# Layer 1's first sequence begun half by half, the contexts' keys behind the first scores, and another order of layer 0's units

## The chip, the cores and the metric

The kernel runs on one NeuronCore of a Trainium2 chip, as one launch. The metric is the device time of the launch in microseconds (us), lower is better. PE is TensorE (PEld its weight loads), DVE is VectorE, ACT is ScalarE, POOL is GpSimd, SP is SyncE, which here only issues DMAs.

## The reference

A decoder of two layers over 16 sequences of 256 tokens of width 128 in f32, each sequence with a context of 64 rows of width 96. Every block is `x = layernorm(x + block(x))`. Cut to what is computed:

```python
x = ln(x + self_attn0(x))         # 16 heads of 8, causal
x = ln(x + cross_attn0(x, ctx))   # 8 heads of 16
x = ln(x + moe0(x))               # 64 experts, top 6, at most 64 tokens each, plus a shared expert
x = ln(x + self_attn1(x))         # 16 heads of 64, causal, with biases
x = ln(x + cross_attn1(x, ctx))   # 16 heads of 64
x = ln(x + nested_ffn1(x))        # attention, 8 heads of 16, per-quarter widths
# moe0: scores = softmax(x @ gate_w.T); idx = top_k(scores + gate_b, 6)
#   xb[e, pos] = x[token]; h = silu(xb w1) * (xb w3); yb = h w2
#   y[token] += yb[slot] * weight;  z = (silu(x ws1) * (x ws3)) ws2
```

## The kernel before

The program has three stages in time.

**Layer 0** (`contexts` and `layer0(b)`, b = 0 to 15). `contexts` is one program: `context_keys_values` makes the keys (`k0x`, two matmuls of 512 columns) and values (`v0x`, four banks of eight matmuls, each bank followed by eight small copies) of layer 0's cross attention for all sequences; then eight chunks fold layer 1's cross-attention weights with the contexts and store them to DRAM (`gd`, `hd`). `layer0(b)` takes one sequence through self attention (`tp_x`, `qk`, `vp`, scores `s_0a`, `nm_0a`, `p_0a`, ...), cross attention (`s_0x`, ...), the router (`lg`, `sc`, `chosen`, `pos`, `key`, `hit`) and, on POOL, twelve indirect DMAs of 128 rows that scatter its tokens into the experts' slots in DRAM (`xb<-x,slots`).

**Experts.** Eight groups of eight experts: the tokens are read back (`xe<-xb`, only after all scatters), turned (`xet`), multiplied (`eh`, `yp`) and stored (`yb<-ye`). The shared expert runs in eight groups g of 512 tokens: `shared_hidden(g)` makes `hs` (PE `sh`, ACT, DVE), `shared_out(g)` makes `z` and adds it to `x2`; groups 0 to 3 go before the experts, 4 to 7 behind them. The experts' weights `e1, e3, e2` are loaded on SP into the pool `fe`, which opens when layer 0's pools close.

**Layer 1** (`layer1(b)`). POOL gathers each sequence's expert outputs by twelve indirect DMAs (`ge<-yb,slots`), DVE combines them (`xr`, twelve instructions), then layernorm (its power on POOL, `rs_0f`), transposition (`tp_x`, `x3T`), queries, keys and values (`qk`, `vp`), `xpb_1a` on POOL, scores `s_1a`, softmax (`nm_1a`, `p_1a`) and the rest. SP loads the folded weights of a sequence (`gx<-gd`, `hx<-hd`, 1 MB together). The small product `bv_out`, added to `l1_bout`, folds the value bias into the output bias, once.

**What sets the order.** PE, DVE, ACT and POOL run each their instructions strictly in the order in which they stand in their queue. Within layer 0 and within layer 1 that order is written out: each program is recorded as units (neighbouring instructions of one engine), and a string (`ORDER0`, `ORDER1`) names, letter by letter, the program and engine whose next unit comes. Between the separate `manual_schedule` blocks (experts, `bv_out`, layer 1) the compiler's scheduler merges; SP's order it chooses everywhere. A pool that opens on memory of closed pools waits for their last users. Pools lie as a stack; in layer 0 they are, from below, `xt` (with `x2T`, the contexts, the shared expert's weights), `fw` (folding and router tiles, `hit` among them), `kx0`, `x0`. Layer 1's tiles of 4 KB (`v1`, tag `kb4`, 18 buffers) lie on `xt`, `fw` and `fe` and so wait for the shared expert's end.

Of the kernel before, what the change touches and what calls it, by code (L numbers as in the profile page):

```python
# [10 lines left out]
F32 = mybir.dt.float32  # L11
# [23 lines left out]
    ',\'#\'#$#$+$(#)($()*#*))$(*)*)()*))*())*)()*(*()*#*$#*#$**($**(#*)#$%(\'\'$%()\'\')(()*()*(1*)0-#.*((*-**.-(*..(*)#*'  # L35
    '**(///%.(*-/%).(.#/)#/.+.)+/($)-\'/$%.(%\'\'-)\'-./(/./()/--.*#./)(/-)*65/($-*2#)/#/.3(-*$2%).3((442))*-33$43\'\'.4-'
    '-./-./-/.((*/-)(-/)#//+-$/)-\'/.(/2)//%\'3(34-)33*4-)2;:/4.43(-)224242)+4)7.#+3#%34#3+438404$2.0\'4-))27.4%3+8-92'
    '92.%3+8\'3-3-.22/))2+34.4-.+42/23/-47.4-842))+/4#.+4-$-.42\'./324-4-/74.9))%+89\'8+-829.98082.97)+@493-82?7.39-77'
    '.5/87359<9.29#9-.97#.03823908289237984=7$2.7.0433078748293979828497.7.038922937340$<9=79=22978<4932.9.03#9>7>0'
    '=$>%=\'>\'57<938..00=2=7>#382>#3:=#.4.08>730EA%%8<:%=B>$D=\'2\'37<<><><353>A8=7=5>=7>85><>=B9<A>873#9358>C#C%5=B97'  # L40
    'B$<C%<8\'\'=B$C7=<\'\'9<3>35<8=>77>8<85=<9=#>7>$79<>87>A3358>5>=>B:<BC<8#B>73#3>58BC$75<8C$\'9<A>8C%37\'85JAACACA8:='
    '#BBC:BCB<I=CF#CBC?AG=?C<88A%F=CG%:<HFH=#BG:G$<H%G\'\'<H=AA8>8:B=<=:A>ACAB>ABC<C=#CB8C8:<B>AC=<$C:<=\'A=>AC<<A>C=<'
    'BCFC=C%8:8\'GAGH:GGH?AF=CHB88:HG<:OAF=B<HNFF=>GDFGHK=H#HHBD<H=AHF%=?=BGAB?HGAL$?AB\'\'FKHGCFLFM=M=?BBA?CGFCGABHFF'
    'HGHAGC=HF=?BAGAHBFBC?LFHAHAKFLCHBKHGH==?HMLLMA?FBMKLDHLMBLAM=K=?BLAMBK?LLCFLMBMMFKHM=AB?TKMP#MSMKBDGMLFQKPGMDP'
    'LRQKIRKLGIQLFKBBDMGLFKGDLMFMLFGMKQHK$KMBFBDGMKHG#MDK$HFMG#MFLMK$HMPB\'BDMGR%QRD\'QFQFRKGGQHQRFBBFDK#HMRGLD$FK\'PG'
    'RLI%PG\'NPRBFBPRDGPLFQKDYGHLQKNRUGR#RX#LRQ%FGRK%KGPIGL#IQM#QRLIL%K%PMVM$KURG\'G\'ILUWWQKVIPMLPQVV$WV\'\'WQKKLPLMGPG'
    'RIQKRKPQMRPLIQKPRLPR#NRRLUGRGI$RQRIVKVPWPLKVR#LVM#GRGILWPIW$KLWPRU%GI_LQPVUQUNWUWVUWZVNVW#VSW[QSWWPLLUQW$NP$\'\''
    '%UZQW\'\'NV[P]][P^QUULRLNVQPQNURUWUVRUVWPWQZWVPLRLNWUQVPWPWQUQN[UR#WUWVPWP#RWLLNQWPUN]Q%%[S]QPUZQWLLNV[NdP[]U`Q#'
    'VcR[X]#Q]VXP%QU%QSQVZ[aS]$[\'U\'SZVZ[]U][]UV]ZZQQW`S[]VU]ZVSW]U[`WaZ]V]b[bUQZQWS[ZVaa$Sba\'\'b[UUVZVW[Z]U[]UZ[W]ZQ'
    'ZQSV]UZV]S#]]`X$]V][]QQSaUZVbZaSUa#]VaW#$]VbZbUQVSiZe]#bh#V%X[$%Z`[%\'\'Xf^a``[^b`baZb`[VZVXba#[baZXbabZ[b`$]`eb'  # L50
    '\'\'[%ZVgVeX[]#gXaZ]f`%#[a%Zf]`$[\'f\'VgVXfagZZ[`X[]a`b`abZabZ$]b`[\'\'Z`bVVX[`bebXb^ab`b[Zbf`V#bVX[fgZf#Xn[f]`$gm[`'
    'g#$Zbg[je%[^[a$`fe\'\'^eagege^fg#fgcfgac#g[[gf`#a^$g`k\'e%a^%\'`%`aejg[b[#^fkll`a%^eaeb$bf\'a\'e[[e^fgefgegf^`fg`kbe'
    'gaeg``gaea[b[^#g%`^$`ebfgj\'\'ag`kjgaglkcl[k^sealkrkl`keoag`lfaepjfblahjjljlfh`aejoaqcfqkeflckeklefloljkgklaaecf'
    'ljfgclekgpjjfkkegaajcfkelffeckjgkleplpejgljfejlaacfjlloclhlflkqepjfqjalaecpljfgpcpqfjloqkpqaacpeqfjcxooqowqokq'
    'thpmpqffhkqjqpoqkhpuqmjotkqffhpjuvvujhkotpoluvkkjolflofhpoqkqohqjppqjplkqoujqjqkokfoflhqjjohlqkjpqtqkqvmuofvfh'
    'kuuhvjoktuqvpvujoftkhplttvktrvvprjkokmpuopvmuovuvuvopvkqktmpopmtqvouqttpuuotqktkvmptuvoopvtpmutquvooqvtpvovptv'
    'kmktvuvmvvtrptovutpkokmupmqpwuwokkptmmutrutpprrtuvtuuvtpvprurtvuttuuvpprttrvutuwpprutrutuvuptprurwpurwuuwwuuuu'
    'uuwuuwwwwwww'
)
ORDER1 = (  # L60
    '&\'&$&$&&$&$$&$+,#$#+$)#%&#%+#$%$#$%)#%+#%#%#%$+$#%$$#$#)%+#$)#$$%)010$%$&.%+$#$&)%($&#)%$$(&%$%)+%($$&*$$&)#*('
    '%0.(*#*(%%0(%(*(*$$*)&(*))#&)*6)#)%0.(%#0($)#;.5*##%#$5%#$%(.%$$%($&$%)%&$%)&#$*)&3*#0))#+#.%#))%-+%.(%0%*53#*'
    '5(%#*)-$+$(/&-).*)+(/$-*)&#$*(5))#*))**$#*+$%+-/$%-&/$-/$&#/%$(5(*))..#*.(%.+.%$%+#$&)3-&$.#/:3#%-%3#/.5:-$-/3'
    '-.&8-/:($.)(&()*5($*(&*82*:)#)$*-)*)*3+*).+#)./($+/+..(%0(..*(*(0*2*3:#*$2/3(8/:-*..4480(0-.-/)-)&/-/2.3/2+..0'
    '/2)/..(042)/3(3/.30)44(4)*2)*#)4)-$/-$%2$%$2)%2%2.303/-34844:#.8#$#%$#%#$%2$$%73%-8%%%.--./-/-/#/.#.70%./.70/$'
    '8/-8/.09#.#/$0$#%#%#%-%--/-/#//#92%$3#3-4$+43+32+4335(43(&*5$2*(33\'@*5)*/5-)4+)32+.(.42*0(42:7.*3534(843?34-47'
    ')47.389+-39809)5-.+57)/.+795(.7/9)079.(.90-(?)/-2*)/.2/4?(4./)2)*)0*)-?3*.8*87.8(=08?()(*()*()*7)?*7)=*--*8(*='
    '*2=9//3(2*3242)4=24-?433534(3425.4+43=((43(*5)()*2*52*24<024=(4.470.08(<8*9)-=<.=9-88:-.92.8/8:>(842)9:+<>83:3'
    '<>)57=>,E03=58778D92793792988:3929D934<34<>D3<>3<><3>57>88578=9=:-=98=9:-../:./.7D././.--./D-./-8/B22/B<D/<=/B'
    '/<4=7/B447478>29398593797885298-89:34B-2/9:7.48:9--9.D.-/8-:B/-/2/737?979759-93-A/<.5B35=-=7>.5>==<09=.?>=1J7?'  # L70
    '>=?<8<8I>2<>3A==2=>3:2>A?84A>3:CB<CBI7C8A>B7BC==8?>7I89A89AC8:AC8A:C87CI<9==<=B>B2B?>=B>23?343?43<3I434322=432'
    '42I34G7A9G799848:A484GA:4B747G<9G9CIC=<<=><G><>7>==?>2==>?8>2AD4>=<3B?=?2>233:<42>824<4<<>:2>F>8A4G:B7BFC82GCB'
    'B<DCBBD274CB3D78F98F>BGHD<GHHF==:2HA3?G5=AB?A3CACB<6NOAC=FCB<BGCD=CC<N=>HF=>FN=HF=HFHBBADHBGCGA?GCB7=C?78D89D8'
    '98AN8989877B987N9789L<<>LF9FGN9L9F97G>L>A9>H=A7ACB?9C<BC=C8?BBAA=CB<BDC<L>ADCCNB7D78>87CBL7D979<99A=AICACA?C7C'
    '=7K9F8?L=?G7GAH8?HGGF:HGGI8<HIFG;T=<IC=AHS>GGGF<BHBFHIK=HLKDGGHIFBMKGHGDHALKBILHAGLIMGMBMIKBCKSMKBMCKLMB<DMLLD'
    'F==F>S=>K=L>KQK>SL<QHHM<=SF>===<MG<=S><Q>K>ALB>>A>ABF>CQCGCFCFBHAHGDHBHAGDG<BCGGI<AQ>KCI=SLALMQM<LB<N<>=N<=>L<'
    '>PDLFL>FNBH<HHFQDHGIBMGFIFFHL<PDHQ>NHA=FHB<HF=MDHKL?RN=@YXLKKLMFMMXMKLGAGMPBKCILPRMNLGPMLIFQRPMGNLQFQRNRLQGNFG'
    'HXAGHPBPGRIPGRIPRGFXRFHAQHQHQABHXBCBCBKBCKBXCBABCAGMACAGICFBCVICPGCVCFFQCPVPMVRKHQHVFLXVKGSILKKLMKGMKMAMILALUN'
    'GCMBPMLLNMVMILQNALQKRBNBRQQASAACQQASCKCKCKMKMAMMAFUCRGBVFGMAKRBIHQWPQMDSBQKE_SQ^PLPLRPRFRPGNURQQ^ULRKRQQURLVUR'
    'QSVKVWQVNWLWSWKLSMUSLMULWNULWNUWL^UWKVKVMFVMV^MGFMGHGHGF^GHPGHGPGR^FLRPHGHLHFQNHF[KHN[HH[UHL[KKWU[MMK^V[PLXNQP'  # L80
    'PQRFLRRFZPQHNRPQSGRULRQQSR[RNQVSFQVFWFSGGFHFVVPXHHHWFFRPVVXHPWGPPKRFLZRGRNKRVLWKIZLXMPG]]V[JXd[URcVUUcVWPWaWWU'
    'cUWZWQQZ]VVZ]SVVWZXQWPV[SZQ]V[X]P[][XQPXQRcZQRZQ]UQ]SUWQSKW[cULLMLMPLPcVZM[aKM[RLKRKMLKMLKMPLLMaRZQMZMMaSUM[aR'
    ']QcUUWVSUWVUWKQaWVKVPXMWPVV`XWLUaWRVXWKKLLKWVKXMKMUMUMURPWWWUQK^WSK`MLQKbULSZNWQaSLSOi[U[]h]P[`VV`QbX[`b^V]P[['
    'XQP]^U`VQhZR[b[abaaa[Z^Z[]Uf]^]Vh]UVWZVZWh`]V]`bV`bXV`bXZ[b[[Z^[]aU]a^U[aP][f^WWQU^WQRQhRQ`VR`aRPXfWh]QPbQPRPQ'
    'RPQRZVRQXVR[UR`fRUaRPfWPZRhWQf[ZZ[]U]]]Z[[^ZV]PP]cP]QQPX[[PR^e[RV`R^R]fX[V^PaaXPbefURVgZQbaacPbaZacZQZ]XZ]aU]V'
    ']US]ecWQbZVTnmfga`]caZmak``b`mb`be[[beaab^eaabceb[fZcbae[fgZcafgfgg[^gZc[]me[]e[g`[g^`b^[Ubmf`VVWVWUVmaWfVWVUV'
    'UWUVWUVWZkeWkZWefWk]Ugk]`]mW[Wa^U`Wa]``Vb[Zbbk^ba`acZ[baeabcbZf`]acb]UaUcbVVUWUWUW`W`Zbb`[`hbUb^Uj[WeV^k[Uf^`V'
    'g^febffXghVgYsf`fhgrfeaZaegj[gffZhlfgZ[hegj[c]efgfhegagfecfklhZgfkgh[`gja]r[`[][]aer]fabjlfjbahljalckjlkkcjlkk'
    '`rklpa`ZbraZZ][Z]Z[]jr[[]j[ljk]pj]lek]p]pefegefgepgZgrfZf`h]fgfge[hpgZgfhZ[[ZgfZ]hZ]e]e]egegZbgZ`]b[gabZcea[cj'
    'ag^r[_kekll`kf`fmobjkmbkklmpjhlkjm`flkkmlkljoahljkkcolklamelomqofqkqceqkplmafecfg`jagkpmjplp`fl`ahjbaf`khfeeag'  # L90
    'oabaobaofbobpopgpeqpgqfg`qfhqqf`ah`baeb`ab`aoabopbobbep`bqjggk`jbkjljaljlelkkmlk`kljmflclk``bk`mba`abjmbj`llhl'
    '`jfbjlolahfhp`pjqahqppocqparpdelrjpfqropproqkekqqopmofoqgkeqjppmqokqrppfjqrpqkrqjklopklrkmokmkopjpqolpoqoqjljp'
    'prqqpeprqqfoqpfrlpflrokqoqkomqokqfmqoggjjqoggeplpljfrfpokreegepmgfogkgopgmpqegepqgkrpmoprqjpmoqokfqqpgjprjkrol'
    'pqkjfokeqoklkklpjlkrgljkjkljlfjklepelegfrefgkepggerlrljllojepglofkpojjqpoklkoppqpqpopqefqoopqhoqpjqfjpiqjpqqoq'
    'qoqlploolppoqoqoqjqjolkjokqpmopkrnps'
)


class Ref:


    def __init__(self, make):
        self._make, self._made = make, None
# [82 lines left out]
def kernel(ctx: ExitStack, tc: tile.TileContext, a: dict, out: bass.AP):  # L186
# [775 lines left out]
    def widths():  # L962


        for t in (f_nb, f_mask, f_ow, f_ob):
            nc.vector.memset(t, 0.0)
# [325 lines left out]
```

## Time and profile before

| what | value |
|---|---|
| times | 1653.58, 1656.78, 1649.14, 1655.27 us; median 1654.43 |
| profiled execution | 1655.69 us, its span 1653.9 us |
| busy, share of span | PE 90%, PEld 65%, DVE 75%, ACT 67%, POOL 50% |
| layer 0 | 0 to about 598 us (last slots made), scatters to 615 |
| experts, shared expert | 596 to 701 us, overlapping both neighbours |
| layer 1 | first gather at 674, first softmax at 728, end at 1654 us |

All times below are us from the start of the span. Every engine operation is recorded through one helper, so lines all read L141 and groups are told apart by the names of the tiles, without sequence numbers. A row of windows gives, for a stretch, its length, the busy time of PE, PEld, DVE, ACT and POOL (with instruction counts), the granted TensorE clock, the share of the 16 DMA engines and GB/s. A row of the timeline gives start, length, engine, operation, tiles, count and, in brackets, the idle time before and what ended it. A row of the chain gives start, length and what ran.

### The profile page before, as it was taken

What the parts mean: (1) busy time and instruction counts of PE and PEld (TensorE: products, weight loads), DVE (VectorE), ACT (ScalarE), POOL (GpSimd) and SP (SyncE); (2) the same over time, 40 slices, a digit from 0 to 9 for tenths busy, and PEclk for the clock granted to TensorE, in tenths of its full rate; (3) what the DMA queues carried; (4) which work ended last, traced back from release to release, by engine and by line L of the source; (5) the groups of instructions that cost most, each with busy time, mean ns of one, the idle gap of its engine ahead of it and who ended that gap; (6) DMA issues with size and microseconds to landing.
All of it is one profiled execution on the core that took longest, in us unless ns stands there. A gap on an engine that the chain in (4) does not pass through costs nothing.

```text
span 1653.9 us, 36931 instructions
## 1 busy us (share of the span) xinstructions
PE 1485.7 (90%) x12738; PEld 1077.8 (65%) x12738; DVE 1246.3 (75%) x3788; ACT 1107.4 (67%) x3811; POOL 830.7 (50%) x910
## 2 busy tenths in 40 slices
PE   7998989989987678778999999999999999999986
PEld 4665655555555348456777777777778677777764
DVE  5789978978888752345878879868887797788675
ACT  3886778758777321145676778777677767786766
POOL 2144444444444450456827567655666576564441
PEclk9999999989999778779999999999999999999999
DMA  4111110111200057385202232222423322230000
GB/s 141 60 46 34 62 32 27 47 50 37 66 15 2 1 162 198 37 124 51 26 16 29 41 41 36 32 38 17 49 40 44 30 36 40 40 21 5 5 1 11
DMA packets 117190, 73.89 MB, mean 45 GB/s; under 512 B 46555, under 2 KB 106808, under 8 KB 116877
## 3 DMA queue, kind: packets, MB, share of 16 engines
q1 hardware_dynamic: 104717, 58.55, 13.0%
q0 software_dynamic: 12288, 13.00, 11.5%
q8 instruction: 102, 1.67, 0.4%
q14 instruction: 83, 0.68, 0.2%
HBM read 48.05 MB, written 35.65 MB: 51 GB/s over the span
## 4 chain that ended last, share of the span: by engine, by line
PE 44%; DVE 27%; ACT 9%; issue 7%; POOL 6%; DMA 6%; SPq 1%; POOLq 0%; DVEq 0%; ACTq 0%
PE s_1a L141 4%; DMA ge<-yb,slots 4%; PE qk L141 3%; POOL ge L141 3%; ACT p_0a L141 3%; PE o_1a L141 3%; PE s_0a L141 3%; DVE nm_0a L141 3%; PE ptp_1a L141 3%; PE ptp_1f L141 2%; PE pj_1x L141 2%; PE ptp_0a L141 2%; DVE nm_1a L141 2%; DVE x L141 2%; PE vp L141 2%
## 5 line engine op out<-in xcount | busy, mean ns | idle before, releaser
L141 POOL DMA_INDIRECT xb<-x,slots x192 | 189.2, 985 | 258.3 <-DVE hit L141 208.3
L141 ACT ACTIVATE p_1a<-s_1a,nm_1a 128x256 f32<-128x256 f32 (+1 forms) x512 | 211.0, 445 | 68.1 <-DVE nm_1a L141 58.8
L141 POOL TENSOR_TENSOR p_1a<-p_1a,ri_1a 128x512 f32<-128x512 f32 x192 | 197.3, 1039 | 104.5 <-DVE ri_1a L141 90.2
L141 ACT ACTIVATE p_0a<-s_0a,nm_0a 128x256 f32<-128x256 f32 (+1 forms) x512 | 211.7, 453 | 34.5 <-DVE nm_0a L141 34.2
L141 POOL DMA_INDIRECT ge<-yb,slots x192 | 195.6, 1019 | 53.7 <-issue 49.9
L141 ACT COPY pT_1a<-ptp_1a 128x512 f32<-128x512 f32 x192 | 105.9, 619 | 56.7 <-PE ptp_1a L141 56.3
L141 DVE TENSOR_REDUCE nm_1a<-s_1a 128x2 f32<-128x512 f32 (+1 forms) x192 | 126.1, 673 | 19.2 <-PE s_1a L141 19.2
L141 DVE TENSOR_REDUCE nm_0a<-s_0a 128x2 f32<-128x512 f32 (+1 forms) x192 | 125.0, 683 | 11.3 <-PE s_0a L141 11.0
L141 PE MATMUL qk<-x3T,l_wqkv 128*128 128x256 f32 x512 | 126.0, 388 | 2.8 <-DVE r1a L141 1.4
L141 ACT ACTIVATE p_1f<-s_1f,nm_1f 128x256 f32<-128x256 f32 x256 | 119.8, 507 | 11.5 <-DVE nm_1f L141 11.2
L141 PE MATMUL ptp_0a<-ident,p_0a 128*128 128x128 f32 x768 | 111.0, 280 | 13.7 <-ACT p_0a L141 8.1
L141 ACT ACTIVATION_READ_ACCUMULATOR p_0a<-s_0a,nm_0a 128x1 f32 x512 | 122.0, 238 | 0.0
L141 ACT COPY pT_0a<-ptp_0a 128x512 f32<-128x512 f32 x192 | 106.5, 617 | 21.9 <-PE ptp_0a L141 21.5
L141 ACT ACTIVATION_READ_ACCUMULATOR p_1a<-s_1a,nm_1a 128x1 f32 x512 | 117.7, 230 | 0.0
L141 PE MATMUL ptp_1a<-ident,p_1a 128*128 128x128 f32 x768 | 100.8, 275 | 11.1 <-POOL p_1a L141 7.3
L141 DVE SCALAR_TENSOR_TENSOR xr<-ge,slot_w,xr 128x128 f32<-128x128 f32 x160 | 61.0, 381 | 64.1 <-DMA ge<-yb,slots 60.7
L141 PEld LDWEIGHTS qk<-x3T,l_wqkv 128*128 128x128 f32 x512 | 95.2, 196 | 19.9 <-issue 6.1
L141 PEld LDWEIGHTS ptp_0a<-ident,p_0a 128*128 128x128 f32 x768 | 85.7, 142 | 33.7 <-ACT p_0a L141 20.6
L141 PE MATMUL s_1a<-kT,qT 64*128 64x256 f32 (+1 forms) x1024 | 101.4, 339 | 5.2 <-ACT p_1a L141 5.0
L141 PE MATMUL o_1a<-pT_1a,v 128*64 128x128 f32 x1536 | 97.1, 278 | 3.3 <-ACT p_1a L141 1.2
L141 PEld LDWEIGHTS ptp_1a<-ident,p_1a 128*128 128x128 f32 x768 | 87.1, 142 | 16.1 <-POOL p_1a L141 8.9
L141 PEld LDWEIGHTS o_1a<-pT_1a,v 128*64 128x64 f32 x1536 | 85.4, 139 | 18.5 <-issue 3.4
(258 smaller groups left out, 3686.8 us busy)
## 6 DMA issues: line engine op xcount, KB each, us to landing
gd<-g1x_sb SPq DMA_DIRECT2D x32, 256.0 KB
hd<-h1x_sb SPq DMA_DIRECT2D x32, 256.0 KB
gx<-gd SPq DMA_DIRECT2D x16, 512.0 KB
hx<-hd SPq DMA_DIRECT2D x32, 256.0 KB
xb<-x,slots POOLq DMA_INDIRECT x192, 2.2
ge<-yb,slots POOLq DMA_INDIRECT x192, 4.2
e<-in_w1T SPq DMA_DIRECT2D x8, 352.0 KB
e<-in_w3T SPq DMA_DIRECT2D x8, 352.0 KB
```

The lines of the kernel that those rows point to most:

```text
L141: r = f(*[made(x) for x in a], **{n: made(x) for n, x in k.items()})
```

## The change

1. **Start.** The first sequence's tokens and `l0_wqkv` are loaded first; the clearing of `xb` (2 MB of zeros) and of `yb`'s last row moves from SP into ACT's queue; the contexts and their weights come next, the shared expert's weights last. In `ORDER0` PE's queue begins with the first sequence's `tp_x`, then `k0x`'s first matmul, `qk`, `vp`, `k0x`'s second, the first scores, and then the four `v0x` banks; before it began `k0x, k0x, v0x, tp_x, v0x, qk, vp, v0x, scores`. SP fetches the tokens one or two sequences further ahead.
2. **`ORDER0`.** Beyond the start, units are exchanged with near neighbours in many places on all four engines, more of them towards the end. At the end PE now has the last sequence's transposition `tp_x` (of `x1`) ahead of the sequence before's `pos`, and behind that `pos` only the last sequence's 14 remaining units; before, `lg` and `pos` of the sequence before stood ahead of that transposition.
3. **Pools.** `fw` becomes one of layer 0's own pools, so `fe` lies on `fw`, `kx0` and the foot of `x0`; before it lay on `kx0` and `x0`. `v2` (gathers) and `vaf` open with the experts, on the right side; `vaf` is cleared on DVE in `widths` instead of on POOL behind the experts.
4. **Layer 1's first sequence.** One manual block holds everything from the experts on. The gathers of sequence 0 come first, `bv_out` and its addition into the shared expert's tail, then sequence 0 in two halves of 128 tokens: combine, norm, turn, queries, keys and values of each, with matmuls and evictions of 128 columns instead of 256.
5. **`ORDER1`** is, on every compute engine, the old order with the units that item 4 took out missing at its front (PE 13, DVE 17, ACT 10, POOL 7); five neighbouring pairs on DVE are exchanged, and on SP the loads of one more sequence stand ahead.

```diff
-    ctxT = load("ctxT", ...)
-    fw = pool_of(phase_ab, name="fw", bufs=2)
-    ws1 = load("ws1T", ...)
...
     with ExitStack() as phase_a:
+        fw = pool_of(phase_a, name="fw", bufs=2)
...
+        tokens0 = tokens(0)
         l0_wqkv = load("l0_wqkvT", [D, 3 * D], pool=x0_pool)
+        nc.scalar.dma_start(
+            xb.rearrange("(s p) d -> p s d", p=P),
+            zero.unsqueeze(1).to_broadcast([P, NSLOT // P, D]),
+        )
+        nc.scalar.dma_start(yb[NSLOT : NSLOT + 1, :], zero[0:1, :])
+        ctxT = load("ctxT", [DC, B, KV], pool=xt_pool)
...
+    vaf = [wc.tile([P, 2, 8, 32], F32, tag=f"vaf_{i}", name=f"vaf_{i}") for i in range(2)]
+    v2 = pool_of(name="v2", bufs=2, side="right")
...
+    def normed_half(b, i, x, r):
...
+        nc.vector.bn_stats(st, r[:, i, :])
+        nc.vector.bn_aggr(mv, st)
+        nc.vector.tensor_scalar(mv[:, 1:2], mv[:, 1:2], EPS, None, ALU.add)
+        nc.gpsimd.tensor_tensor(rs, mv[:, 1:2], neg_half[:, 0:1], ALU.pow)
+        nc.vector.tensor_scalar(x[:, i, :], r[:, i, :], mv[:, 0:1], rs, ALU.subtract, ALU.mult)
...
+    bv = value_bias()
+    gathered(0)
+    hs5 = shared_hidden(5)
+    shared_out(4, hs4)
+    hs6 = shared_hidden(6)
+    shared_out(5, hs5)
+    hs7 = shared_hidden(7)
+    add_value_bias(bv)
+    r_0 = combine(0, (0,))
...
+    normed_half(0, 0, x_0, r_0)
+    shared_out(6, hs6)
+    turned_half(0, 0, x_0, xT_0)
+    shared_out(7, hs7)
     phase_ab.close()
...
+    queries_of(0, 0, x_0, xT_0, *qkv_0)
+    combine(0, (1,))
+    normed_half(0, 1, x_0, r_0)
+    turned_half(0, 1, x_0, xT_0)
+    queries_of(0, 1, x_0, xT_0, *qkv_0)
```

`queries_of` makes, for one half, four banks of four matmuls of 128 columns, evicts eight blocks on DVE (`qT`) and eight on ACT (`kT`), and two banks of 512 columns for the values, one copied by ACT and one by DVE. `turned_half` is one transposition and one copy; `combine` is the old loop of six instructions per half.

## The prediction, before the run

> **What bounds the kernel now.** I read the windows by stage first, to see where engines are idle at all, since a change of order can only win idle time.
>
> ```profile
> 0.00:20.00 20.00, 12.50 (x66) 8.19 (x70) 8.07 (x31) 2.24 (x4) 9.46 (x30) 1.00 0.73 209
> 200.00:300.00 100.00, 88.35 (x781) 54.74 (x779) 84.47 (x308) 73.64 (x276) 43.51 (x49) 0.97 0.11 32
> 560.00:600.00 40.00, 19.33 (x70) 9.64 (x70) 26.35 (x132) 6.50 (x17) 19.25 (x21) 0.62 0.13 33
> 690.00:705.00 15.00, 6.37 (x26) 5.81 (x27) 6.14 (x16) 0.00 (x0) 4.88 (x5) 0.50 0.48 38
> 705.00:735.00 30.00, 21.06 (x110) 15.15 (x108) 14.52 (x39) 10.51 (x36) 15.08 (x16) 0.78 1.05 137
> 1200.00:1400.00 200.00, 192.51 (x1762) 151.74 (x1759) 158.86 (x441) 148.43 (x503) 126.36 (x137) 1.00 0.31 39
> ```
>
> From 800 us on PE is busy 94 to 97%; that stretch keeps its order, and I expect it only to shift. In the middle of layer 0 PE (88%) and DVE (84%) bind together. Idle time lies at four places: the start (PE idle 7.5 of 20 us, ACT nearly wholly), layer 0's end (PE 20.7 of 40), and 690 to 735, where PE is idle 17.6 of 45 us and ACT sleeps. The chain of waits says who ends each.
>
> ```profile
> 4.47 2.68 DMA l0x_wk<-in_l0x_wk
> 7.20 3.78 PE k0x L141 x4
> 10.98 1.91 PE v0x L141 x16
> 12.88 0.62 PE tp_x L141 x2
> ...
> 689.53 6.37 issue
> ...
> 701.93 4.97 issue
> ...
> 720.85 12.92 DMA ge<-yb,slots
> ```
>
> At the start the contexts' weights and matmuls stand ahead of the first sequence. At the turn of the layers the chain runs through POOL's gathers: POOL stands 6.37 us (for sequence 0's last gathers, behind its power) and 4.97 us (`xpb_1a`, behind `bv_out`), and then DVE waits for gathers in flight. Third, the timeline at three places.
>
> ```profile
> 22.03 0.37 ACT L141 ACTIVATE p_0a<-s_0a,nm_0a 128x128 f32<-128x128 f32 x1 [0.56 <-DVE nm_0a L141]
> ...
> 567.51 0.23 PE L141 MATMUL pos<-chosen,upper 128*128 128x64 bf16 x1 [5.75 <-DVE chosen L141]
> ...
> 594.23 0.34 SPq L141 DMA_DIRECT2D e<-in_w1T  x1
> ...
> 720.05 2.06 PE L141 MATMUL s_1a<-kT,qT 64*128 64x128 f32 x32
> ...
> 727.67 0.35 DVE L141 SCALAR_TENSOR_TENSOR xr<-ge,slot_w,xr 128x128 f32<-128x128 f32 x1 [0.98 <-DMA ge<-yb,slots]
> 727.94 1.28 DVE L141 TENSOR_REDUCE nm_1a<-s_1a 128x4 f32<-128x512 f32 x2
> ```
>
> The first exponential runs at 22.03. The last sequence's chain stands behind a `pos` that waits 5.75 us. Layer 1's scores are there at 720 to 725, but its first softmax waits for 727.67: the last gather of sequence *1*, whose combination stands before it on DVE.
>
> **Start.** The tokens' issue moves from 7.30 to about 0.8; landing then took 3.0 us (`xpb_0a` at 10.33), so `tp_x` starts at about 3.8 instead of 12.8, and `xT` is there at about 5.5 (DVE's 1.77 us cast stands before it until then). `k0x`'s first matmul is now queued between `tp_x` and `qk` and waits for `l0x_wk`: issued fourth, at about 2.2, landing 2.68 later, so 4.9 if undisturbed, some 2 us later beside the zeros. It costs half of 3.78 us, 1.9. `qk` then runs from about 7.5, and from `xT` to the first exponential there were 7.8 us (14.23 to 22.03), of which 1.1 was a `v0x` bank before `qk`: the first exponential comes at about 14, 8 us earlier. That is not all won. Up to 33 us PE was busy 23.2 us (12.5 of the first 20, and 10.7 in the windows after), and the same work started at 3.8 cannot end before 27: at most 6 us earlier. Between 8 (if ACT's softmax decides) and about 2 (if PE stalls on the contexts) I take 5, near the PE sum's end, because PE is busy 36 of the 40 us from 20 to 60.
>
> ACT now issues the zeros. On SP the second of these issues lasted 5.28 us, which ACT will be held for, to 8 or 10 us; its first work (`kx`) is due at about 9. Cost 0 to 1, taken 0. A rule speaks against this move: the Trainium skill ("DMA: Bandwidth & Descriptors", Issuing engines are not separate DMA queues) says that DMAs of SP, ACT and POOL run on the same 16 DMA engines and interleave. By it the zeros share the engines with the first loads instead of following them; the row of 0 to 20 us, DMA share 0.73, leaves room. If all 2 MB stood ahead of the contexts, the gain at the start would be near 0 instead of 5; the zeros' issue behind two loads makes that the far end.
>
> **Layer 0's order.** At the end, `pj_0a` of the last sequence finishes at 561.2, its `x1` needs 0.3 (`r0a`), 0.9 of statistics, 0.74 on POOL and 0.6, so 564 to 564.5; it came at 567.97, behind the sequence before's router on DVE and its `pos` on PE. That exchange is worth up to 3.6 us; I take 3, since the delayed router must still end before the last scatters. The other exchanges can't be priced one by one. PE is idle some 53 us between 60 and 560 (by the windows), in waits of 1 to 6 us; one exchange moves a wait of this size either way. I take 0, with 8 down (a sixth of the idle) and 8 up.
>
> **Pools.** The experts' weights were issued at 594.23, just after `sb` (593.77 and 0.29) read the last tile of `x0`; `fe` now also covers `fw`, whose last user is the last `hit` at 600.3: 6 us later. About 6.6 MB follow at full DMA share until 619.4, then `xe` is issued, and PE takes up `xet` at 622.3. If the weights shift by 6, `xe` queues behind them: cost 5.5. If SP issues layer 1's 2 MB of weights, which don't lie on `fw`, in the gap, cost 0. The compiler chooses SP's order and has already put constants ahead (the loads at 19.9 us); I take 2. `vaf` on DVE is under 1 us where DVE is busy 12.83 of 46: nothing.
>
> **Turn of the layers.** The last `yb` store is issued at 671.25 and gathers start at 674.14 as before. PE's tail without waits: `sh` to 684.1 as now, then `bv_out` (16 records; 3.75 at half clock, 1.9 at full) to 686. DVE: the first half's six combinations 686.5 to 688.2, statistics to 689; the power waits until POOL has issued all twelve gathers (689.53), so the first half is normed at 690.8. Last `z` at 693.1; that frees `v1` (701.3 before). The first half's queries: 8 DVE and 8 ACT evictions of some 0.35, the value copies 0.6 and 0.7: to 697.7. Second half's combination and norm 3.7, turning 0.7, queries again 4.5: 706.5, instead of 718.7 with `vp`'s copies. The scores come about 13 us earlier. Added are 8 DVE and 8 ACT evictions, about 2 us on each; they lie in this stretch, where ACT was busy 0.00 of 15, and cost nothing; without that cover, 2.
>
> But the first softmax still stands behind sequence 1's gathers. POOL is in order: it can start these only after the second half's power, at about 701, and then needs 12 x 1.305 and `xpb_1a` 0.72: issue ends at 717.5, as before (717.9). Before, the last landed 9.7 us after its issue, because `gx` and `hx` (1 MB per sequence, four sequences) held the DMA engines from 701 to 735 (share 1.05). They now start when `v1` is free, at 693, and end some 8 us earlier. The last gather lands between 722 (lag as at 708) and 728 (12 at the contended 1.86 us each, from 707). I take 726.5; the next gathers (sequence 2's, awaited until 733.8) gain about as much. Turn: 2.5 won, from 3 lost to 8 won.
>
> On the clock: it was granted at 0.50 from 688 to 709, after PE's idle stretches. The Trainium skill ("TensorE: Matmul & The Clock Gate", HAM oscillation) asks for no idle gap over 3.4 us; the new gaps are by my list 2.9 and 4, so part of the halves would run slow, for perhaps 2 us, hidden behind the gathers.
>
> **Sum**, against the profiled execution's 1655.69 (span 1653.9 and 1.8 around it; 1.3 above the median): start -5, end of layer 0 -3, other exchanges 0, weights +2, turn -2.5: -8.5, so 1647.2, and 1645.9 on the median. I say 1646.
>
> **The rivals.** (1) *The wins are absorbed*: PE's lead from the start is lost in layer 0's in-order waits, the weights come the full 6 us late, and the gathers land when they did: -5 -3 +5.5 -0 leaves 2.5 won, 1652. For it: the chain passes POOL and DMA, not PE. Chance 0.21. (2) *All wins carry through*: 8 at the start, 3.6 at the end, 6 by the exchanges, 8 at the turn: 1629. For it: idle time of that size is there. Against it: DMA at share 1.05. Chance 0.12. (3) *Slower*: the new order of layer 0 fits other durations than the chip's, and units placed early wait at the head of PE's and DVE's queues. Place: 60 to 560 us, where waits of DVE on ACT and of PE on DVE are 0.5 to 6 us. It decides once it adds more than the 8.5 won and the 5 of measurement, a quarter on the 53 us of idle; with 20 added, 1666. For it: some 150 of 694 places in PE's queue hold another unit. Against: most are swaps of neighbours. Chance 0.15. The forecast has 0.52.
>
> **Numbers.** About 0.3% (5 us) is what a measurement of this kernel can tell from no change: faster is below 1649.4. The forecast's own range, 1639 to 1653, lies about four fifths below this (0.42); with rival 2 (0.12) and a third of rival 1's spread (0.08), 0.62 faster. Same gets the rest of both, 0.23; slower 0.15. The range for 8 in 10 leaves out about 0.08 below and 0.12 above: 1635 to 1660.
>
> **What would show it.** Right: first exponential at 13 to 16; last `slots` 6 to 10 us before 597.5; first `s_1a` about 12 us earlier against the last `yb` store, but first `nm_1a` only 1 to 4 us earlier against it. Wrong: `xet` over 30 us behind the last `slots` (24.8 now), more PE idle than 53 us between 60 and 560, or `nm_1a` directly behind the scores.

## The result, and the profile after

The change makes the kernel slower by a little: 1657.5 us (median of 42 runs, 1653.2 to 1662.6) against 1652.5 for before in the same series (69 runs). The ratio is 1.0031, with a 95% interval of 1.0023 to 1.0038, so 5.1 us, 3.8 to 6.3. The forecast was 8 us the other way. The profiled execution after took 1659.70 us, its span 1657.4 (before 1655.69 and 1653.9).

The windows of after, in the stretches shown of before (length, busy time of PE, PEld, DVE, ACT and POOL, granted clock, DMA share, GB/s):

```profile
0.00:20.00 20.00, 10.51 (x74) 6.51 (x76) 7.99 (x23) 5.02 (x20) 9.46 (x30) 1.00 0.70 205
200.00:300.00 100.00, 88.08 (x757) 55.30 (x755) 86.25 (x307) 74.81 (x279) 45.27 (x49) 0.97 0.11 35
560.00:600.00 40.00, 22.27 (x158) 12.87 (x159) 25.31 (x119) 11.53 (x33) 18.72 (x21) 0.70 0.05 10
690.00:705.00 15.00, 10.52 (x53) 9.21 (x53) 7.04 (x21) 3.20 (x9) 1.80 (x3) 0.77 0.92 120
705.00:735.00 30.00, 13.40 (x93) 10.33 (x93) 9.37 (x28) 4.55 (x10) 17.36 (x18) 0.74 1.07 117
1200.00:1400.00 200.00, 194.39 (x1784) 153.50 (x1783) 160.07 (x441) 144.91 (x491) 124.47 (x135) 1.00 0.29 38
```

The halves do fill 690 to 705 (PE busy 10.52 of 15 us, 6.37 before, ACT 3.20 instead of 0.00), but the 30 us after it are emptier by more than that: PE 13.40, before 21.06. Late in layer 1 (1200 to 1400) PE is as full as before: 194.39 of 200 us, before 192.51. The chain of waits (start, length, what ran) says what stands at the start and at the turn:

```profile
2.38 6.73 DMA l0x_wk<-in_l0x_wk
9.25 2.04 PE k0x L140 x2
...
692.13 14.66 issue
722.67 12.48 DMA ge<-yb,slots
```

`l0x_wk` now lands in 6.73 us instead of 2.68, beside the zeros, although fewer bytes were issued ahead of it on SP (704 KB, before 1032). At the turn, POOL stands 14.66 us in one piece ahead of the second half's power, and then the chain goes through the last gather of sequence 1. The timelines of the engines (start, length, engine, operation, tiles, and in brackets the idle time before and what ended it) show what that does:

```profile
17.52 0.37 ACT L140 ACTIVATE p_0a<-s_0a,nm_0a 128x128 f32<-128x128 f32 x1 [0.58 <-DVE nm_0a L140]
...
706.84 0.55 POOL L140 TENSOR_TENSOR rsh<-mvh,neg_half 128x1 f32<-128x1 f32 x1 [14.70 <-DVE mvh L140]
...
716.12 2.06 PE L140 MATMUL s_1a<-kT,qT 64*128 64x128 f32 x32
...
735.24 0.35 DVE L140 SCALAR_TENSOR_TENSOR xr<-ge,slot_w,xr 128x128 f32<-128x128 f32 x1 [1.43 <-DMA ge<-yb,slots]
735.51 1.28 DVE L140 TENSOR_REDUCE nm_1a<-s_1a 128x4 f32<-128x512 f32 x2
...
739.19 1.11 PE L140 MATMUL ptp_1a<-ident,p_1a 128*128 128x128 f32 x4 [17.58 <-POOL p_1a L140]
```

The first exponential comes at 17.52 (22.03 before, 14 forecast). Layer 1's first scores come at 716.12, earlier than before, and then stand 19 us: the first reduce is directly behind sequence 1's last sum of gathered rows, and PE is idle 17.58 us in one piece. Set against the first gather (676.09 after, 674.14 before), the scores come at 40.0 us (45.9 before), but the first reduce at 59.4 (53.8).

In layer 0 the times of `slots` give the lead of the new order at each sequence's end: 4.0 us at the first (85.5, before 89.5), 3.1 at the second, and 1.5 us *behind* at the third (162.4, before 160.9); 2.9 behind at the last (600.4, before 597.5). These are single profiles, and they differ by some us: a second one of the same kernel (e15 below) has the first slots at 82.0, the third at 158.2 and the last at 598.0; it lacks a stretch of half clock, 6.8 us at 50 us, that the first has. In both, about 5 us of the lead are lost between the first slots and the third (5.5 and 4.8).

### The profile page after: what moved, and what is told of

It reads as the page before. It is cut to its first block, busy times and chain, and to the rows that moved or that the text cites. A ratio compares the mean times of both kernels' runs of the same rounds, so it can differ in the third digit from the quotient of the medians.

```text
span 1657.4 us, 37019 instructions
## 1 busy us (share of the span) xinstructions
PE 1482.1 (89%) x12770; PEld 1076.6 (65%) x12770; DVE 1254.8 (76%) x3801; ACT 1111.6 (67%) x3819; POOL 829.7 (50%) x909
## 4 chain that ended last, share of the span: by engine, by line
PE 46%; DVE 25%; ACT 10%; issue 7%; POOL 5%; DMA 5%; SPq 0%; POOLq 0%; DVEq 0%; ACTq 0%
PE s_1a L140 5%; DMA ge<-yb,slots 4%; PE qk L140 4%; ACT p_0a L140 4%; PE s_0a L140 4%; PE o_1a L140 3%; POOL ge L140 3%; PE ptp_1a L140 3%; PE ptp_0a L140 3%; PE ptp_1f L140 2%; DVE x L140 2%; PE pj_1x L140 2%; DVE nm_0a L140 2%; PE s_1x L140 2%; DVE nm_1a L140 2%
## 5 line engine op out<-in xcount | busy, mean ns | idle before, releaser
L140 PE MATMUL qk<-x3T,l_wqkv 128*128 128x256 f32 (+1 forms) x544 | 128.5, 381 | 1.9 <-DVE r1a L140 0.8
L140 PEld LDWEIGHTS qk<-x3T,l_wqkv 128*128 128x128 f32 x544 | 98.7, 202 | 17.8 <-issue 4.9
L140 PEld LDWEIGHTS ptp_1a<-ident,p_1a 128*128 128x128 f32 x768 | 87.4, 142 | 27.2 <-POOL p_1a L140 20.5
L140 POOL TENSOR_TENSOR p_1x<-p_1x,cri_1x 128x512 f32<-128x512 f32 x64 | 66.0, 1045 | 59.6 <-DVE cri_1x L140 40.8
```

What stands on the lines that cost most here:

```text
L140: r = f(*[made(x) for x in a], **{n: made(x) for n, x in k.items()})
```

## Experiments

Three theories. **A**: the loss is in layer 0's new order. **B**: it is at the turn of the layers, where sequence 1's gathers wait for the second half's power. **C**: the start is won nowhere, because the zeros take it back. A difference between two variants below is the difference of their ratios to before, times 1653 us; its uncertainty is the root of the summed squares of the half intervals.

### Taking the change apart: four kernels

`e1_turn_alone`: the kernel after with layer 0 as before.

```diff
-    tokens0 = tokens(0)  ...  nc.scalar.dma_start(xb, zero)  ...  ctxT, l0x_wk, l0x_wv
+    ctxT, ws1, ws3, ws2  ...  l0_wqkv, l0_wout, ...   (old order of loads)
+    contexts(): clear_slots() on nc.sync first
-    ORDER0 = new
+    ORDER0 = old
```

> The kernel after with layer 0 as it was before: the loads at the start in their old place and order, the two clears of the rows on SP's queue again, and the old ORDER0. New are then only the pools and the turn of the layers (sequence 0 half by half, value bias early) with the new ORDER1. Theory A (the loss of the change sits in layer 0's new order): this is faster than before by what the turn was priced at, about 2.5 us, ratio 0.998 to 0.9995. Theory B (the loss sits at the turn, where sequence 1's gathers wait for the second half's power and lie beside the loads of gx and hx): slower by 3 to 5 us, ratio 1.002 to 1.003, with the first nm_1a as far behind the last yb store as in the kernel after (63 us, 57 before). Theory C (the two profiles differ by chance and both parts are near nothing): 0.9995 to 1.0005.

Measured: 1.0014 (0.9998 to 1.0030), 2.3 us lost, 2.6 either way. The turn, with the pools and the new `ORDER1`, does not win its 2.5 us; between the first gather and the first reduce lie 58.9 us here, as in the kernel after.

`e2_layer0_alone`: the kernel before with the loads, the clears on ACT and the `ORDER0` of after.

> The kernel before with layer 0 as it is after: tokens, projections, contexts and key weights loaded first, the clears on ACT's queue, the new ORDER0; the turn of the layers, ORDER1 and the place of fw stay as before. Theory A: the new layer 0 ends later by the 2.9 us that the profile after shows at the last slots, and that carries: ratio 1.0015 to 1.0025. Theory B: layer 0 ends within 1 us of before on the average of the runs, ratio 0.9995 to 1.0005. The on-record sum had it 8 us earlier (start 5, end 3): ratio 0.995.

Measured: 0.9999 (0.9986 to 1.0013). The new layer 0 as a whole wins nothing of its 8 us. And the kernel after, which adds the turn to it, is 5.3 us slower (2.6 either way). So both A and B hold something.

`e3_new_start_old_order` and `e4_old_middle` cut `ORDER0` (2460 units on the four compute engines) at two places where both orders have handed out the same units:

```diff
 # e3: units of ORDER0
   0 to 166: new          # the start, to about 40 us
-  166 to 2460: new
+  166 to 2460: old
 # e4
   0 to 166: new
-  166 to 2049: new
+  166 to 2049: old       # about 40 to 520 us
   2049 to 2460: new      # the end of layer 0
```

> The kernel after with its first 166 units of layer 0 (the start, up to about 40 us) and then the old order of units to the end of layer 0. Against the kernel e1 it differs by the start alone. If an in-order schedule carries a start that is 4 us earlier (first exponential at 17.5 instead of 22.0), it is 3 to 4 us faster than e1, and the slots of the sequences stand 3 to 4 us earlier to the end. If the start's gain is used up by something that does not depend on the order (the transfers of the first 60 us), it is within 1 us of e1 and the lead is gone by the third sequence (161 us).

Measured: 0.9982 (0.9967 to 0.9997); against e1, which has the old start, 5.3 us won (3.6 either way). The last slots come at 590.5 (595.4 in e1). The start's gain carries to the end; theory C falls.

> The kernel after with only the middle of ORDER0 put back: the first 166 units and those from the 2050th on stand as in the kernel after, the units between (about 40 to 520 us) as before. If the new middle costs the 5 to 8 us that the profile shows between the first sequence's slots and the thirteenth's, this is the fastest of the four layer-0 variants, 5 to 8 us faster than the kernel after (ratio to before 0.998 to 1.000). If the new tail alone is worth the 4 us that the profile after regains past 545 us, it is 4 us faster than e3; if that regain is only sequences waiting less after a late middle, it equals e3.

Measured: 0.9970 (0.9957 to 0.9982): 2.0 us below e3 (3.2 either way, so the end alone is not told from nothing), and 10.1 us below the kernel after (2.5 either way). So the four parts are: start 5.3 won, end 2.0 won, middle of layer 0 10.1 lost, turn 2.3 lost. That they add up to the 5.1 measured is by construction, each being the step between two kernels of one row.

### The turn: what stands behind what

`e5_half_gathers_first` uses POOL's idle 14.7 us:

```diff
     normed_half(0, 0, x_0, r_0)
+    gathered(1, (0,))          # six gathers of sequence 1's first 128 tokens
     shared_out(6, hs6)
...
-        gathered(b)            # layer 1, sequence 1: all twelve
+        gathered(b, (1,) if b == 1 else (0, 1))
```

> The kernel after with six of sequence 1's twelve gathers (its first 128 tokens, whose buffer is free once sequence 0's first half is combined) put on POOL ahead of the power of sequence 0's second half, so that they go out in POOL's idle time between 692 and 707 us. If sequence 0's first reduce (nm_1a) waits behind sequence 1's sums of gathered rows on DVE, as the trace after shows (PE idle 17.6 us from 721.6), the last gather goes out about 7 us earlier, and nm_1a follows by 4 to 7 us: ratio to before 0.9995 to 1.001, where the kernel after has 1.0031. If the transfers of gx and hx set when the gathers land (1.8 us apart whatever their issue), nm_1a moves by under 2 us and the time by under 1 us: 1.0025 to 1.0035.

Measured: 0.9988 (0.9975 to 1.0001), 7.1 us below the kernel after (2.5 either way), somewhat more than expected. POOL's timeline and DVE's:

```profile
692.41 1.06 POOL L140 DMA_INDIRECT ge<-yb,slots  x1 [0.18 <-issue]
...
706.70 0.57 POOL L140 TENSOR_TENSOR rsh<-mvh,neg_half 128x1 f32<-128x1 f32 x1 [6.68 <-DVE mvh L140]
...
725.27 0.35 DVE L140 SCALAR_TENSOR_TENSOR xr<-ge,slot_w,xr 128x128 f32<-128x128 f32 x1 [1.94 <-DMA ge<-yb,slots]
725.54 1.28 DVE L140 TENSOR_REDUCE nm_1a<-s_1a 128x4 f32<-128x512 f32 x2
```

The power of the second half is where it was (706.70), six gathers went out before it from 692.41, and the first reduce comes 10 us earlier, still behind the same sums. Sequence 0's transposed `x4T` comes 104.3 us behind the first gather (113.9 after, 109.1 before).

`e6_gx_hx_held` takes the loads of `gx` and `hx` out of the gathers' way:

```diff
-    nc.sync.dma_start(gx, ...)
+    nc.sync.dma_start(gx, ..., then=behind sequence 1's twelve gathers)   # sequences 0 to 3
```

> The kernel after with the loads of gx and hx of sequences 0 to 3 held until sequence 1's twelve gathers have landed; the gathers are issued from the same place as in the kernel after, in program order just behind the power of the second half. If the gathers land late because those 4 MB lie on the same DMA engines, they land 2 to 3 us behind their issue instead of 12.5 and nm_1a comes at about 726 instead of 735.5: 5 to 9 us gained there, ratio to before 0.998 to 1.001, unless gx of sequence 0 is then late for its scores (needed at about 775, loaded by about 745: it should not be). If the gathers are paced by their own packets, no change: 1.0025 to 1.0035.

Measured: 1.0024 (1.0009 to 1.0039), 1.2 us below the kernel after (2.8 either way), so the second theory's numbers. DVE's waits for gathered rows:

```profile
729.12 0.35 DVE L140 SCALAR_TENSOR_TENSOR xr<-ge,slot_w,xr 128x128 f32<-128x128 f32 x1 [1.13 <-DMA ge<-yb,slots]
730.98 0.35 DVE L140 SCALAR_TENSOR_TENSOR xr<-ge,slot_w,xr 128x128 f32<-128x128 f32 x1 [1.50 <-DMA ge<-yb,slots]
...
750.77 0.35 DVE L140 SCALAR_TENSOR_TENSOR xr<-ge,slot_w,xr 128x128 f32<-128x128 f32 x1 [6.59 <-DMA ge<-yb,slots]
```

With no other load beside them the gathers still land 1.5 to 1.9 us apart (1.6 to 2.5 in the kernel after). The last lands 4.3 us earlier, at 730.98, 9.2 us behind its issue (12.5 in the kernel after); 0.9 of the 4.3 is that here it is issued ahead of `xpb_1a`, at 721.78 instead of 722.67. But the held loads then lie beside sequence 2's gathers, for which DVE waits 6.59 us in one piece (3.78 in the kernel after), and the 4.3 us are given back. The contention is real but small, and moved rather than removed.

`e7_seq0_first_round_ahead` and `e8_seq0_two_rounds_ahead` change only places in `ORDER1`:

```diff
 # DVE's queue; PE, ACT and POOL likewise
-  sums of sequence 1's rows (4 units), sequence 0's reduces and reciprocals
+  sequence 0's first 8 units (e7) or 16 units (e8), sums of sequence 1's rows
```

> The kernel after with one change in ORDER1: sequence 0's first eight units on DVE (with those of PE, ACT and POOL between them) stand ahead of sequence 1's first unit on DVE, which is the sum over its gathered rows. So nm_1a of sequence 0 no longer waits for sequence 1's gathers. Theory B in its sharper form (the earlier scores win nothing because the next step stands on DVE behind sequence 1's gathers): first nm_1a at 717 to 718 instead of 735.5, PE's idle stretch of 17.6 us shrinks to under 8 in one piece, and 3 to 8 us are gained at the end: ratio 0.998 to 1.001. If sequence 1 is what the following steps wait for, whatever sequence 0 does, the gain is under 2 us: 1.002 to 1.003.

> As the run before it, but with both of sequence 0's rounds of scores (16 units on DVE) ahead of sequence 1's sums. If DVE has time to spare until sequence 1's rows have landed (735 us), this is at least as good as the smaller move: 0.997 to 1.001. If the sums and with them the gathers of sequence 2 (they wait for the buffers that the sums set free) come too late, it gives some of that back: 1 to 4 us slower than the smaller move, with DVE's waits for gathered rows at 750 to 775 us longer.

Measured: e7 1.0024 (1.0008 to 1.0039), 1.2 us below the kernel after; e8 0.9992 (0.9981 to 1.0003), 6.4 us below (2.3 either way). DVE's first reduce and PE's next long wait, in e7 and then in e8:

```profile
718.98 1.29 DVE L140 TENSOR_REDUCE nm_1a<-s_1a 128x4 f32<-128x512 f32 x2 [1.61 <-PE s_1a L140]
740.58 0.66 PE L140 MATMUL tp_x<-ident,x 128*128 128x128 f32 x2 [14.71 <-DVE x L140]
```

```profile
714.42 1.29 DVE L140 TENSOR_REDUCE nm_1a<-s_1a 128x4 f32<-128x512 f32 x2 [1.61 <-PE s_1a L140]
736.50 0.66 PE L140 MATMUL tp_x<-ident,x 128*128 128x128 f32 x2 [12.62 <-DVE x L140]
```

In both the first reduce is 17 us closer to the first gather than in the kernel after, directly behind its scores. In e7 that is worth nothing: PE then waits 14.71 us for sequence 1's normed rows, since behind the first round its queue holds sequence 1's units. In e8 PE still waits 12.62 us there, but more of sequence 0 is done by then (PE busy 48.6 of the 50 us from 740, 44.1 in the kernel after). So my sharper form of theory B is half right: an earlier first softmax alone wins nothing; what counts is when sequence 1's rows come, or how much other work is placed ahead of them.

### The middle of layer 0, and a faster version

`e9_old_first_part`: the kernel after with units 166 to 716 of `ORDER0` (about 40 to 162 us) old, all others new.

> The kernel after with ORDER0's units 166 to 716 (about 40 to 162 us, the end of the third sequence's slots) put back as before, and the rest new. The whole old middle (units 166 to 2049) made the kernel after about 10 us faster. If the loss sits in the first sequences (the profiles: 77.0 us from the first to the third slots, 71.4 with the old middle, part of it a dip of the granted clock), this wins 4 to 6 us of it: ratio to before 0.9995 to 1.001. If it is spread evenly (per unit), it wins 29%, about 3 us: 1.001 to 1.002. If it sits behind, under 1 us: 1.0025 to 1.0035.

Measured: 0.9987 (0.9973 to 1.0001), 7.3 us below the kernel after (2.6 either way). That is more than the 4 to 6 expected for a loss in the first sequences: most of the middle's 10 us lies in this stretch, 29% of its units.

`e10_middle_and_gathers` is e4 and e5 together, `e11_and_seq0_ahead` adds e8's places, `e12_old_turn_new_ends` is the kernel before with e4's layer 0.

> The old middle of ORDER0 (as in e4_old_middle, ratio 0.997) together with six of sequence 1's gathers ahead of the second half's power (as in e5_half_gathers_first, 4 us below the kernel after). They lie in different stages. If both carry, 4 us below 0.997: 0.994 to 0.995. If layer 1 sets its own pace from the first gathers on, the second gives 0 to 2 us: 0.996 to 0.997.

> e10_middle_and_gathers and, besides, both of sequence 0's rounds of scores ahead of sequence 1's sums on DVE (as in e8_seq0_two_rounds_ahead). Both edits remove the same wait of nm_1a for sequence 1's gathers, so the gains do not add: within 2 us of e10, ratio 0.993 to 0.996. If sequence 1 is then late (its sums stand behind 16 units of sequence 0), up to 3 us slower than e10.

> The kernel before (its turn of the layers, ORDER1 and place of fw) with the new start and the new end of ORDER0 and the old middle, that is the layer 0 of e4_old_middle. Against e4 it differs by the turn alone. With the new turn priced at 2.3 us lost (e1) to 5 us lost (the kernel after against e2), it is 2 to 5 us faster than e4: ratio 0.994 to 0.996. If the turn is near nothing, 0.9965 to 0.9975.

Measured: e10 0.9934 (0.9917 to 0.9951), e11 0.9930 (0.9912 to 0.9948), e12 0.9941 (0.9921 to 0.9961). e10 is 6.0 us below e4 (3.5 either way): the two gains are of different stages and both carry. e11 is level with it, as expected of two cures for one wait. e12 against e4 prices the new turn once more, at 4.8 us lost (3.9 either way). With its gathers reordered (e10) the new turn is no worse than the old one, and not measurably better either. e10, 1643.0 us where before took 1654.2, beats both kernels by 0.7% (before) and 1.0% (after).

### Waits or clock?

In the profile of after, this first part of the middle looks like this at its worst place: PE's two waits, then the windows around them.

```profile
154.22 0.33 PE L140 MATMUL tp_x<-ident,x 128*128 128x128 f32 x1 [1.41 <-DVE x L140]
...
157.63 2.07 PE L140 MATMUL s_0a<-kx,qT 32*128 32x512 f32 x2 [1.78 <-DVE x1T L140]
```

```profile
153.00:155.00 2.00, 0.78 (x4) 0.67 (x7) 1.94 (x5) 2.00 (x8) 1.75 (x2) 1.00 0.11 29
155.00:157.00 2.00, 0.84 (x6) 0.01 (x1) 1.83 (x9) 0.16 (x1) 1.80 (x3) 0.86 0.01 0
157.00:159.00 2.00, 1.37 (x2) 0.50 (x2) 2.00 (x5) 0.80 (x5) 0.08 (x1) 0.50 0.38 125
159.00:161.00 2.00, 2.00 (x11) 1.12 (x11) 1.00 (x5) 0.71 (x5) 0.00 (x0) 0.50 0.52 203
```

DVE is full (1.94 and 1.83 of 2 us), PE is busy 1.62 of 4 us, and the granted clock falls to 0.50 from 156.4 to 163.2. What DVE is full with is not another order: from the fourth sequence's `x1` over the third's router (`sc` to `chosen`) to the copy `x1T` its instructions are the same, in the same order, as before. What moved is on POOL, as the rows of after and then of before show:

```profile
152.03 2.13 DVE L140 TENSOR_SCALAR x<-r0a,mv_0a,rs_0a 128x128 f32<-128x128 f32 x2
153.01 1.06 POOL L140 TENSOR_TENSOR kx0x<-kT0x,hm 128x512 f32<-128x512 f32 x1
```

```profile
152.98 0.60 DVE L141 TENSOR_SCALAR x<-r0a,mv_0a,rs_0a 128x128 f32<-128x128 f32 x2
155.38 1.38 DVE L141 TENSOR_TENSOR chosen<-rp,sb 128x128 bf16<-128x128 f32 x1
155.53 1.06 POOL L141 TENSOR_TENSOR kx0x<-kT0x,hm 128x512 f32<-128x512 f32 x1
```

The new order has `kx0x` and `xpb_0x` one scatter earlier in POOL's queue, and so `kx0x` runs beside DVE's two `x`, for which PE's `tp_x` waits; before, it ran later, beside `chosen`. The second `x` lasts 1.87 to 1.88 us in all eleven profiles with this stretch of the new order and ends about 0.1 us behind `kx0x`; in the nine with the old stretch it lasts 0.34 or 0.35. The 242 DVE instructions that in before ran from 85 to 161 us take 81.5 to 82.1 us in the eleven, 79.1 to 79.4 in the nine. No run exchanges these POOL units alone, so what this one exchange costs is not shown.

The dip of the clock begins 69 to 74 us behind the first slots in the profile of each kernel with this stretch that does not fill the wait, and in none of those with the old stretch and the new start. (e1, with the old start, has a short one at 68 us.) It was open whether the waits or the clock cost the 7 us. `e13_filled_wait` puts work of no use into the first wait; `e14_new_first_part_alone` puts the new stretch into e10.

```diff
     def transposed(x, dst, name, fill=0):
         for i in range(2):
+            for _ in range(fill if i else 0):       # fill=6 for sequence 3's x1
+                nc.tensor.matmul(t[:, 2 * P : 3 * P], ident, ident, start=True, stop=True)
             nc.tensor.transpose(t[:, i * P : (i + 1) * P], x[:, i, :], ident)
```

> The kernel after with six matmuls of no use (identity by identity, 128 columns, about 0.28 us each) ahead of the second transpose of sequence 3's x1, where PE waits 1.41 us for DVE at about 153 us. Clock theory (a few us with PE mostly idle make the granted clock fall to half from 156.7 to 163.2 us, and that costs some 3 us): the clock stays at 1.00 there, first to third slots take 73 to 75 us instead of 76.2 to 77.0, ratio to before 1.001 to 1.002. Wait theory (the clock follows something else, and the loss is the waits): the dip stays, the stretch takes 76 to 77.5 us, ratio 1.003 to 1.0035. The second gap, 1.78 us at 155.8, is not filled; if that alone is enough for the dip, the wait theory's numbers come out too, and the run does not tell them apart.

> The fastest version (e10_middle_and_gathers, 0.9934) with ORDER0's units 166 to 716 as in the kernel after and the other middle units as before. If this stretch costs 7 us whatever surrounds it: ratio 0.9970 to 0.9980, first to third slots 76 to 79 us with a dip of the clock in them. If its price came only with the rest of the new middle: 0.993 to 0.995.

Measured: 1.0098 (1.0070 to 1.0125) and 1.0014 (0.9994 to 1.0035), on a chip where before took 1686 us. There PE stands 20.5 us (e13) and 17.9 us (e14) in waits for nothing that the profile shows; 2.4 to 3.0 in all other profiles. Neither has its base on that chip, so the times settle nothing; in e13's profile the dip is gone. I ran both again, each beside its base.

> The kernel after, unchanged, as the base for the filled wait on this chip. Expected: its ratio to before as over all its runs, 1.002 to 1.004, with a dip of the granted clock 70 to 80 us behind the first slots and 76 to 78 us from the first to the third slots.

> The kernel after with the six matmuls of no use in PE's wait at about 153 us, beside its base. Clock theory: the dip 70 to 80 us behind the first slots is gone, the stretch is 2 to 3 us shorter, and the time is 1 to 3 us below the base (ratio lower by 0.001 to 0.002). Wait theory: no dip is removed, or it is removed without gain; the time is that of the base or up to 2 us above it (the six matmuls last 1.7 us at full clock).

> The fastest version (old middle of ORDER0, six of sequence 1's gathers first), unchanged, as the base for the next run. Expected: 0.992 to 0.995, first to third slots 71.5 us without a dip (75 with one).

> The fastest version with ORDER0's units 166 to 716 as in the kernel after, beside its base. If this stretch costs the same 7 us whatever surrounds it: ratio above the base by 0.003 to 0.005, first to third slots 76 to 79 us. If its price came only with the rest of the new middle: within 0.0015 of the base.

Measured: e15 1.0028 (1.0010 to 1.0045), e16 1.0010 (0.9988 to 1.0032), e17 0.9932 (0.9911 to 0.9954), e18 0.9959 (0.9940 to 0.9978). The windows of e15, of e16 and of e17, from the first slots on and around the dip:

```profile
82.00:158.00 76.00, 64.53 (x544) 39.18 (x543) 64.41 (x222) 51.35 (x191) 34.63 (x37) 0.95 0.13 41
150.00:162.00 12.00, 10.60 (x41) 7.07 (x42) 9.76 (x35) 5.57 (x21) 5.14 (x6) 0.57 0.16 55
```

```profile
82.00:158.00 76.00, 65.77 (x575) 41.62 (x574) 65.22 (x230) 53.62 (x198) 34.62 (x37) 1.00 0.13 41
150.00:162.00 12.00, 10.19 (x77) 5.95 (x77) 11.53 (x41) 7.63 (x28) 5.65 (x7) 1.00 0.16 55
```

```profile
82.00:158.00 76.00, 68.28 (x595) 42.00 (x594) 66.74 (x236) 56.27 (x209) 37.29 (x40) 1.00 0.13 41
150.00:162.00 12.00, 11.50 (x111) 8.07 (x113) 11.73 (x40) 10.66 (x37) 4.96 (x6) 1.00 0.11 37
```

In e15 the clock is 0.57 over the 12 us around the dip; in e16, with 1.5 us of work in the first wait, it is 1.00. From the first slots to the fourth they take 107.2 us (e15), 104.3 (e16) and 100.7 (e17). So of 6.5 us lost to the fourth slots, 2.9 went with the dip, which the waits caused, and 3.6 are left where the clock is full. The 2.9 are not the clock's alone: in e16 PE's second wait also comes later, behind the scores, and is 0.74 us instead of 1.40. In the rows of 76 us PE is idle 11.5, 10.2 and 7.7 us. In the time the filled wait shows as 3.0 us (4.7 either way), which alone would say nothing; the two profiles with the filled wait (e13, e16) against the nine without it do. e18 against e17 puts the stretch at 4.5 us (4.8 either way), in agreement with the 7.3 and on its own not told from nothing.

## Why the prediction was wrong

**The step that failed first: "other exchanges 0".** The middle of layer 0 costs 10.1 us, just outside the 8 I allowed. I read "most are swaps of neighbours" as a reason for nothing either way. But PE and DVE are both busy 84% and more here, and a swap also changes what runs beside an instruction: at the worst place DVE's second `x`, for which PE waits, takes 1.88 us instead of 0.34, in every profile together with an exchange on POOL, and the stretch's DVE instructions together take 2.4 to 3.0 us more. The clock then added to it, which I had applied to the turn alone. My own sign, PE idle between 60 and 560 us, came out (62.5 us, 53.0 before) but does not tell: e4, with the old middle, has 58.2, and e10, the fastest, 61.3, all three with the new start, which brings more of layer 0's emptier end into that window. Rival 3 had the place, and PE that waits at the head of its queue; I had priced it at 20 us added and given it 0.15. It needed to add only some 13 to be slower, and the middle's 10.1 with the turn's failure did.

**The second: the turn, 2.5 won.** It loses 2.3 to 5.3 us, by three pairs of kernels (the old or new layer 0, or e4's, around it). I had the queue right: the first softmax stands behind sequence 1's gathers, and these behind the second half's power. Mis-sized was the power, 701 by the sum and 706.84 by the trace: the last `z` ran at about half clock (0.53 from 692 to 697) to 696.5 instead of 693.1, and the first half's evictions, which I had at 4.5 us, lasted from 698.2 to 703.8, DVE and ACT each waiting up to 0.48 for the other's. And the last gather landed 12.48 us behind its issue, where I took 9, because I gave the pace to `gx` and `hx` and had them end earlier; e6 shows it is mostly the gathers' own, 9.2 us with those loads held back. So it lands at 735.24, not 726.5. The range for the turn, from 3 lost to 8 won, reached to about there; the value I took from it did not. That four of sequence 1's gathers had gone out at 697 to 702 before, in POOL's idle time ahead of `xpb_1a`, and could no longer, was in the trace of before, and I did not price it.

**Right: the start, 5 won** (5.3 by e3 against e1), though by luck in one step. The first exponential came at 17.5, not 14: `l0x_wk` took 6.73 us beside the zeros, where I took 2.68 and some 2 us. The zeros went out at 1.09, behind one load and not behind two. The Trainium skill ("DMA: Bandwidth & Descriptors", Issuing engines are not separate DMA queues) speaks of just this interleaving, and this row agrees with it, though no run takes the zeros away alone. It did not matter, because I had not taken the 8 us of the first exponential but the bound by PE's work. **Near, but not told from nothing: the end, 3 won.** The times give 2.0; in the profiles the twelfth slots are 141.5 to 141.6 us ahead of the last scatter's issue with the old end (before, e1, e3) and 139.2 to 141.3 with the new one (e13 and e14, on the other chip, apart), so 0.2 to 2.4. **Mis-sized: the weights, 2 lost.** `xet` comes 24.4 us behind the last slots, 24.8 before: nothing. The experts' weights were issued 6 us later against the last slots, as I had it, but SP put layer 1's weights into the gap (597.2 to 598.5), the case that I had given as costing 0.

**The clock.** The Trainium skill ("TensorE: Matmul & The Clock Gate", HAM oscillation) asks for no idle gap over 3.4 us. I weighed only gaps near that size. Here two waits of 1.41 and 1.78 us, with 1.62 us of work in four, were enough for half clock, and in e16, which fills the first and delays the second, it stayed full. The measured rows decide. In the 20 profiles, between 60 and 560 us, every stretch of half clock lasts a whole number of 3.41 us. Cut at this step, all 58 pieces at full clock with PE busy under 45% were followed by half clock, although in 57 of them PE was idle no longer than 2.7 us at a time; of 1761 with PE busy 86% or more none was; between the two, 65 of 860 were. So here it is the busy share of some 3.4 us, not the longest gap.

Two things stay open. Where the other 3 us of the middle lie (units 716 to 2049), I did not try, nor which single exchanges make up the 7. And a dip is not certain where PE's share lies between: e3 and e11 have the old first part and show one of their own 35 us behind the first slots (75.0 us to the third instead of 71.4).

## What to carry to other kernels

When a unit is moved earlier, ask on each engine what is queued directly behind it and what will now run beside it on the others, and follow those; the win of an earlier step (scores 6 us earlier) is worth what its next step's place in its queue allows. In a stage where two engines are both nearly full, price exchanges of neighbours with a loss in the range as large as this one's (10 us for 1883 units), and count the clock that short waits in a row will cost. Take a planned change apart at points where both orders have issued the same work: the parts here (5 and 2 won, 10 and 2 lost) leave only 5 lost in their sum, and the won ones could be kept.

## What the runs showed of the hardware

- The granted clock fell to 0.50 for 6.8 us, at the end of 3.4 us in which PE was busy under half of the time, with no wait over 1.8 us; with six small matmuls in the first wait it stayed at 1.00. The stretches of half clock in layer 0 last 3.41 us or a multiple of it.
- A DVE instruction of 0.34 us (`x`, 128x128) lasted 1.88 us where POOL ended a scatter and ran `kx0x` beside it, and ended 0.1 us behind `kx0x`, in all eleven profiles that place them so.
- Gathers of 128 rows, issued 1.3 us apart, land 1.5 to 1.9 us apart with the loads of `gx` and `hx` held back, and 1.6 to 2.5 with them.
- From the last slots to the first gather, the profiles of the first three series took 71.2 to 79.7 us, though the experts' part is nearly the same in all of them; single profiles can't price a few us there.
